# A selective scan with a mixture of experts: softplus by the logarithm, a share as a bias, and small products on two halves at once

## The chip, the cores and the metric

The kernel runs on one core of a Trainium2 chip. The metric is the time of one execution on the device in microseconds (us). A core has five engines that work side by side: PE (TensorE, matrix products), DVE (VectorE), ACT (ScalarE), POOL (GpSimd, here only issuing gathers and scatters) and SP (SyncE, issuing plain transfers). Each engine runs its own instructions in order; semaphores make one wait for another.

## The reference

The input x has 2 batches of 2048 tokens with 256 features. The result is x plus two branches of the normalised tokens. Cut to what matters:

```
xn = layernorm(x)
# branch 1: a scan over each batch's tokens, sorted by the nearest of 8 cluster means
prompt = (means @ prompt_weight.T)[bucket]         # 16 numbers per token
x_dbl  = x_proj_weight @ u                         # u: sorted tokens, (256, 2048); gives 32 + 16 + 16 rows
dts, Bm, Cm = x_dbl[:32], x_dbl[32:48], x_dbl[48:] + prompt.T
delta  = softplus(dt_projs_weight @ dts + bias)    # (256, 2048)
for t:                                             # 16 states n for each of 256 channels
    h = exp(delta[t] * A) * h + delta[t] * u[t] * Bm[t]
    y[t] = sum_n h * Cm[t] + D * u[t]
# branch 2: 8 experts, each token uses its best 2
probs = softmax(top-2 logits)
out = sum_k probs_k * (silu(xn @ w1[k]) * (xn @ w3[k])) @ w2[k]
```

Sorting is by a stable argsort of the bucket, so a batch's sorted tokens are eight runs, one per cluster.

## The kernel before

A front part loads x, takes statistics, scores each token against the means and the gate, normalises the rows, sorts, and writes the rows with their expert numbers and two shares to memory (`xn_d`, 260 columns: 256 features and four more). The first of the four is the best expert's number, the second the smaller share, the third the difference of the two shares.

Then two kinds of work run mixed.

**The scan** goes by eight *pieces* of 512 sorted steps (four per batch). For a piece, POOL gathers the rows (`gather`, four indirect transfers), PE transposes them into `u` (`turn`), and PE projects them: `project` (line 652) makes `px`, 64 rows by 512 steps, in two products over the halves of the 256 features, and `end_projection` (659) adds the prompts with a third one, from `member`, a table of 8 clusters by 512 steps that is 1 where the step is in the cluster's run (`find_members`, line 644, two DVE instructions). ACT copies `px` to `xd`; SP stores its last 32 rows to memory (`bc`) and later loads them spread over partitions (`load_b`, `load_z`). `step_size` (685) makes, for each half h of the channels, `pd` = 32-row product of 512 columns, and ACT takes |pd + bias|, relu(pd + bias) and exp(-|pd + bias|) from it. Softplus is relu + log(1 + e), and log(1 + e) is a product of four quadratic factors: ACT makes each square (`square`, 700) and DVE multiplies them up (`series`, 706: five instructions and one more for delta times u), 512 columns at a time, for each of two halves.

A piece has eight *steps* (4 groups of 4 states, times 2 halves of the channels), and a step has four *places*, one per state. At a place ACT makes `da` = exp(delta * A) of the step after (`decay`, six buffers), DVE makes `bu` and runs the scan (`hs`, three buffers); a step later PE transposes `hs` into `pt_s` (two PSUM banks, pool "t"), ACT copies it to `ht`, and PE contracts with `z` into `y`, four products side by side on four groups of 32 partitions.

**The experts** go by 71 *tiles* of 128 rows. POOL gathers weights (`load_up`, `load_down`) into three buffers and rows (`load_rows`) into `xg`, with four buffers: a buffer is written again when all that read it are done. `turn` (854) transposes the rows on PE, ACT copies them to `xT`, and DVE makes `own`, the tile's share per row, in two instructions: the difference where the tile's expert is the row's best, plus the smaller share. `up` makes two products of 16 pairs, ACT takes Tanh of the first, DVE does `silu` and `gate`, `down` makes `py`; ACT scales it by `own` into `yo` and POOL adds `yo` into memory (`add_rows`). The products `px`, `pd`, `pt_g`, `pt_u` and `py` share a PSUM pool "m" of two banks.

**The order** is written out: each engine keeps the order of the text. `at_place` (1029) puts the pieces' preparations at fixed places of the piece before, with costs in us for PE and DVE, and a loop over the places (1076) gives out the tiles' parts (`jobs`: up 0, up 1, and down of the tile before) wherever PE's sum falls behind DVE's. `part_down(t)` turns tile t+2, gathers rows for tile t+5, then does `down(t)` and loads weights for t+3. The first piece is prepared in a *lead* (1000), whose thirteen entries alternate with jobs. When all jobs are given, memory is copied to the output, and the last piece's sums are added to it.

Of the kernel before, what the change touches and what calls it, by code (L numbers as in the profile page):

```python
# [40 lines left out]
F32 = mybir.dt.float32  # L41
BF16 = mybir.dt.bfloat16
I32 = mybir.dt.int32
AF = mybir.ActivationFunctionType
ALU = mybir.AluOpType
# [4 lines left out]
P = 128  # L50
CH = 512
# [4 lines left out]
LOG1P = (  # L56
    (1.0093577, 1.1060627), (-0.08225194, 3.2574694), (-1.424736, 2.702104), (-2.321687, 0.43240654),
)
LOG1P_C = 0.0052326876


@with_exitstack
def scan_moe_kernel(
# [14 lines left out]
    nc = tc.nc  # L78
    B, L, D = x.shape
# [3 lines left out]
    R = dt_wT.shape[0]  # L83
# [9 lines left out]
    SH = 4  # L93
    BJ = B * J
# [26 lines left out]
    last = [cst.tile([K, NCH], F32, name=f"last{b}") for b in range(B)]  # L121
# [80 lines left out]
    log1p_a = cst.tile([P, len(LOG1P)], F32, name="log1p_a")  # L202
    for i, (a, _) in enumerate(LOG1P):
        nc.vector.memset(log1p_a[:, i : i + 1], a)
# [25 lines left out]
    dtT = cst.tile([R, D], F32, name="dtT")  # L230
    nc.sync.dma_start(dtT, dt_wT)
# [41 lines left out]
    def small_weights():  # L273

        diag = cst.tile([P, ND, P], F32, name="diag")
        for h in range(ND):
            nc.vector.tensor_scalar(diag[:, h, :], ident, dcol[:, h : h + 1], None, ALU.mult)

        cp = cst.tile([K, XP], F32, name="cp")
        nc.vector.memset(cp, 0.0)  # L280
        pc = ps_m.tile([K, NS], F32, tag="m", name="pc")
        for h in range(ND):
            nc.tensor.matmul(
                pc, lhsT=chosen_by[:, h, 0:K], rhs=pwT[:, h, :], start=h == 0, stop=h == ND - 1
            )
        nc.vector.tensor_copy(cp[:, R + NS :], pc)

        nc.scalar.activation(na, na, AF.Exp)
        nc.vector.tensor_scalar_mul(na, na, -1.0)
        return diag, cp  # L290
# [146 lines left out]
    def sort_tokens():  # L437
# [56 lines left out]
        for b in range(B):  # L494
            nc.vector.tensor_scalar(first[b], begins, fst[:, b : b + 1], None, ALU.add)
            nc.vector.tensor_scalar(last[b], first[b], cntT[:, b : b + 1], None, ALU.add)
# [129 lines left out]
    class Piece:  # L626
# [17 lines left out]
        def find_members(self):  # L644
            b, c = self.b, self.c
            self.member = scn.tile([K, CH], F32, tag="member", name="member", bufs=1)
            nc.vector.tensor_scalar(self.member, at, first[b][:, c : c + 1], None, ALU.is_ge)
            nc.vector.scalar_tensor_tensor(
                self.member, at, last[b][:, c : c + 1], self.member, ALU.is_lt, ALU.mult
            )  # L650

        def project(self, h: int):
            if h == 0:
                self.px = ps_m.tile([XP, CH], F32, tag="m", name="px")
            nc.tensor.matmul(  # L655
                self.px, lhsT=xpT[:, h, :], rhs=self.u[:, h, :], start=h == 0, stop=False
            )

        def end_projection(self):
            nc.tensor.matmul(self.px, lhsT=cp, rhs=self.member, start=False, stop=True)  # L660
            self.xd = prep.tile([XP, CH], F32, tag="xd", name="xd")
            nc.scalar.copy(self.xd, self.px)
            nc.sync.dma_start(bc_d[self.b][self.c], self.xd[R:XP, :])
# [21 lines left out]
        def step_size(self, h: int):  # L685

            if h == 0:
                self.e = pre.tile([P, ND, CH], F32, tag="tok", name="e")
                self.r = pre.tile([P, ND, CH], F32, tag="tok", name="r")
                self.sq = {}  # L690
            pd = ps_m.tile([P, CH], F32, tag="m", name="pd")
            nc.tensor.matmul(  # L692
                pd, lhsT=dtT[:, h * P : (h + 1) * P], rhs=self.xd[0:R, :], start=True, stop=True
            )
            nc.scalar.activation(self.e[:, h, :], pd, AF.Abs, bias=bias[:, h : h + 1])
            nc.scalar.activation(self.r[:, h, :], pd, AF.Relu, bias=bias[:, h : h + 1])  # L696

            nc.scalar.activation(self.e[:, h, :], self.e[:, h, :], AF.Exp, scale=-1.0)

        def square(self, h: int, i: int):  # L700
            self.sq[h, i] = scn.tile([P, CH], F32, tag="sq", name="sq", bufs=3)
            nc.scalar.activation(  # L702
                self.sq[h, i], self.e[:, h, :], AF.Square, bias=log1p_a[:, i : i + 1]
            )

        def series(self, h: int, i: int):

            if h == 0 and i == 0:
                self.dl = prep.tile([P, ND, CH], F32, tag="dl", name="dl")
                self.du = prep.tile([P, ND, CH], F32, tag="du", name="du")  # L710
            dl = self.dl[:, h, :]
            if i < len(LOG1P):
                nc.vector.scalar_tensor_tensor(
                    dl, self.sq.pop((h, i)), LOG1P[i][1], dl if i else self.e[:, h, :],
                    ALU.add, ALU.mult,
                )
            elif i == len(LOG1P):
                nc.vector.scalar_tensor_tensor(
                    dl, dl, LOG1P_C, self.r[:, h, :], ALU.mult, ALU.add
                )  # L720
            else:
                nc.vector.tensor_mul(self.du[:, h, :], dl, self.u[:, h, :])
# [107 lines left out]
    class Tile:  # L830
# [23 lines left out]
        def turn(self):  # L854
# [11 lines left out]
            nc.vector.tensor_add(self.own, self.own, xg[:, D + 1 : D + 2])  # L866
# [27 lines left out]
        def down(self):  # L894
# [6 lines left out]
            yo = ffn.tile([P, D], F32, tag="yo", name="yo", bufs=3)  # L901
            nc.scalar.activation(yo, py, AF.Copy, scale=self.own)  # L902
# [90 lines left out]
    def first_series(h: int):  # L993
        for i in range(len(LOG1P) + 2):
            if i < len(LOG1P):
                p.square(h, i)
            p.series(h, i)

# [5 lines left out]
        [lambda: p.load_b(0), *(lambda q=q: p.load_z(q) for q in range(NQ)), lambda: p.step_size(0)],  # L1004
        [lambda: p.step_size(1), lambda: first_series(0)], [lambda: first_series(1)],
# [29 lines left out]
    for n, p in enumerate(pieces):  # L1035
# [3 lines left out]
        if n:  # L1039
            s1 = s0 - SP_  # L1040
            at_place(max(s1 - 1, 0), 1 if n > 1 else 0, p.gather)
            for h in range(ND):
                at_place(s1 + 1, 2 + h, lambda p=p, h=h: p.turn(h), 0.5)
                at_place(s1 + 2, 1 + 2 * h, lambda p=p, h=h: p.project(h), 0.95)
                at_place(s1 + 3 + h, 2 - 2 * h, lambda p=p, h=h: p.step_size(h), 1.0)
                for i, place in enumerate(((17, 18, 20, 21, 23, 25), (19, 22, 24, 26, 28, 30))[h]):
                    if i < len(LOG1P):
                        at_place(s1, place - 2, lambda p=p, h=h, i=i: p.square(h, i))
                    at_place(s1, place, lambda p=p, h=h, i=i: p.series(h, i), 0.0, 0.6)
            at_place(s1 + 2, 0, p.find_members, 0.0, 1.2)  # L1050
            at_place(s1 + 3, 0, p.end_projection, 0.95)
# [117 lines left out]
```

## Time and profile before

| | |
|---|---|
| Time, median of 3 runs | 794.46 us (793.4 to 795.9) |
| Profiled execution | 793.45 us |
| Its span | 791.7 us |
| Mean granted TensorE clock | 0.951 |
| PE busy | 712.9 us, 90% |
| DVE busy | 711.3 us, 90% |
| ACT busy | 507.9 us, 64% |
| POOL busy | 520.9 us, 66% |

Busy time counts an instruction from start to end; neighbours overlap, so the distance of two starts is what one really takes from its engine. "Idle before" is the engine's wait just ahead of an instruction, with what ended it. The chain is followed back from the last instruction to what released each one. POOL's rows are issues of indirect transfers; the transfers land later.

The front part lasts to about 67 us, the lead to about 117, the mixed stretch to about 751, and the last scan steps, the copy and the last sums to 791.7.

### The profile page before, as it was taken

Reading aid. Unit: us, or ns where it says so; the run is one execution under the profiler, and the core shown is the slowest. Engines: PE = TensorE matmul, PEld = TensorE weight load, DVE = VectorE, ACT = ScalarE, POOL = GpSimd, SP = SyncE. Lnnn points to the kernel's source line nnn. Section 1 sums busy time; section 2 is a strip of 40 time slices with the busy share of each in tenths; the row PEclk is TensorE's granted clock in tenths of the full one; section 3 lists DMA queues with packets and bytes.
Section 4 is the critical chain, followed back from the end, with each engine's and each line's share of the span. In section 5 each row is a group of like instructions: output and inputs, shape, how many; then the busy total and the mean of one; then the engine's idle time right before and its main releaser. Section 6 shows DMA issues by size and latency. Waiting matters only on the chain.

```text
span 791.7 us, 16967 instructions
## 1 busy us (share of the span) xinstructions
PE 712.9 (90%) x6552; PEld 605.5 (76%) x6552; DVE 711.3 (90%) x1162; ACT 507.9 (64%) x986; POOL 520.9 (66%) x374
## 2 busy tenths in 40 slices
PE   7385979899999999899999999999999998999963
PEld 5144768589877988599868986798779885998842
DVE  8865269899999999899989999899999998899991
ACT  4821266586669657776668666866687576757572
POOL 2023738657867886788776787878678787686313
PEclk9755999999999999999999999999999998999996
DMA  8593244664368547855656367448644855444462
GB/s 280 222 323 114 58 173 108 210 172 97 108 155 244 154 106 215 203 148 143 206 140 176 56 247 219 107 95 263 197 111 132 273 156 112 107 102 96 86 219 27
DMA packets 61215, 125.90 MB, mean 159 GB/s; under 512 B 24464, under 2 KB 42032, under 8 KB 53776
## 3 DMA queue, kind: packets, MB, share of 16 engines
q0 software_dynamic: 40224, 65.03, 34.6%
q1 hardware_dynamic: 20912, 59.80, 22.1%
q8 instruction: 52, 0.85, 0.4%
q14 instruction: 27, 0.22, 0.1%
HBM read 180.06 MB, written 27.00 MB: 262 GB/s over the span
## 4 chain that ended last, share of the span: by engine, by line
PE 69%; ACT 6%; DVE 3%; issue 3%; DMA 2%; POOL 1%; POOLq 0%; SPq 0%; ACTq 0%; DVEq 0%
PE p_ps L875 28%; PE py L898 14%; PE pt_s L787 12%; PE y L796 6%; ACT ht L791 2%; DMA out_dram<-acc 2%; PE y L728 2%; PE pt_g L858 2%; PE px L655 2%; PE pd L692 1%; DVE hs L775 1%; ACT da L760 1%; DVE bu L766 1%; PE px L660 1%; PE pt_u L641 1%
## 5 line engine op out<-in xcount | busy, mean ns | idle before, releaser
L875 PE MATMUL p_ps<-xT,w 128*128 128x128 f32 x2272 | 280.3, 279 | 5.3 <-ACT sq L702 4.3
L875 PEld LDWEIGHTS p_ps<-xT,w 128*128 128x128 f32 x2272 | 268.2, 195 | 20.2 <-issue 9.3
L775 DVE TENSOR_TENSOR_SCAN hs<-da,carry,bu 128x512 f32<-128x512 f32 x192 | 246.2, 1283 | 0.0
L760 ACT ACTIVATE da<-dl,na 128x512 f32<-128x512 f32 x256 | 182.0, 723 | 1.1 <-DVE hs L775 1.0
L816 POOL DMA_INDIRECT acc<-yo,token_of x71 | 137.8, 1941 | 60.3 <-ACT yo L902 20.0
L766 DVE TENSOR_TENSOR bu<-du,bt 128x512 f32<-128x512 f32 x256 | 174.0, 680 | 0.0
L791 ACT COPY ht<-pt_s 128x512 f32<-128x512 f32 x256 | 137.1, 590 | 31.3 <-PE pt_s L787 31.0
L787 PE MATMUL pt_s<-ident,hs 128*128 128x128 f32 x1024 | 137.9, 279 | 14.7 <-ACT ht L791 8.7
L835 POOL DMA_INDIRECT w<-in_w_up_dram,w_row x71 | 94.8, 1335 | 84.2 <-DVE w_row L584 36.8
L898 PE MATMUL py<-w,g 128*128 128x256 f32 x568 | 139.0, 389 | 12.2 <-ACT r L696 8.7
L787 PEld LDWEIGHTS pt_s<-ident,hs 128*128 128x128 f32 x1024 | 117.7, 143 | 31.6 <-ACT ht L791 15.6
L898 PEld LDWEIGHTS py<-w,g 128*128 128x128 f32 x568 | 104.2, 193 | 27.1 <-ACT r L696 10.3
L849 POOL DMA_INDIRECT xg_sb<-xn,token_of x71 | 88.3, 1243 | 37.5 <-issue 30.2
L835 POOL DMA_INDIRECT w<-in_w_down_dram,w_row x71 | 93.5, 1317 | 21.6 <-issue 12.5
L883 ACT ACTIVATE t_sb<-p_ps 128x512 f32<-128x512 f32 x71 | 42.5, 599 | 69.4 <-PE p_ps L875 69.1
L902 ACT ACTIVATE yo<-py,own 128x256 f32<-128x256 f32 x71 | 33.8, 476 | 80.5 <-PE py L898 80.3
L775 DVE TENSOR_TENSOR_SCAN hs<-da,bu 128x512 f32<-128x512 f32 x64 | 78.2, 1223 | 0.0
L796 PE MATMUL y<-ht,z 128*32 128x128 f32 x2048 | 74.3, 279 | 2.5 <-ACT ht L791 1.9
L816 POOL DMA_INDIRECT acc<-yt,line_of x28 | 54.7, 1952 | 25.7 <-ACT ht L791 8.2
L796 PEld LDWEIGHTS y<-ht,z 128*32 128x32 f32 x2048 | 51.1, 110 | 24.5 <-issue 13.2
L888 DVE SCALAR_TENSOR_TENSOR t_sb<-t_sb,p_ps 128x512 f32<-128x512 f32 x71 | 48.2, 679 | 9.1 <-ACT t_sb L883 8.8
L892 DVE SCALAR_TENSOR_TENSOR g<-t_sb,p_ps 128x512 f32<-128x512 f32 x71 | 48.3, 681 | 7.2 <-PE p_ps L875 4.7
(188 smaller groups left out, 632.8 us busy)
## 6 DMA issues: line engine op xcount, KB each, us to landing
bt<-bc SPq DMA_DIRECT2D x32, 1024.0 KB, 5.4
z<-bc SPq DMA_DIRECT2D x32, 256.0 KB, 3.8
xn<-xt SPq DMA_DIRECT2D x8, 520.0 KB, 2.6
xt<-in_x_dram SPq DMA_DIRECT2D x8, 512.0 KB, 7.5
acc<-in_x_dram SPq DMA_DIRECT2D x8, 512.0 KB, 6.4
w<-in_w_up_dram,w_row POOLq DMA_INDIRECT x71
w<-in_w_down_dram,w_row POOLq DMA_INDIRECT x71
xg_sb<-xn,token_of POOLq DMA_INDIRECT x71
```

The lines of the kernel that those rows point to most:

```text
L760: nc.scalar.activation(self.da[i], self.piece.dl[:, self.h, :], AF.Exp, scale=na[:, self.h, n : n + 1])
L766: nc.vector.tensor_mul(self.bu[i], self.piece.du[:, self.h, :], self.piece.bts[self.q][:, i, :])
L775: nc.vector.tensor_tensor_scan(self.hs[:, :, i], self.da[i], self.bu[i], start, ALU.mult, ALU.add)
L787: nc.tensor.transpose(pt[:, j, :], self.hs[:, t0 : t0 + G, :].rearrange("p t n -> p (t n)"), ident)
L791: nc.scalar.copy(self.ht[i], pt)
L796: nc.tensor.matmul(p.ys[self.h][j * G : (j + 1) * G, i, :], lhsT=p.zs[q][:, i * (P // G) + j, :], rhs=self.ht[i][:, j, :], start=False, st ...
L816: ins = nc.gpsimd.indirect_dma_start(out=to, out_offset=bass.IndirectOffsetOnAxis(ap=numbers, axis=0), in_=rows, in_offset=None, compute_o ...
L835: nc.gpsimd.indirect_dma_start(out=to[self.t % NW], out_offset=None, in_=rows, in_offset=bass.IndirectOffsetOnAxis(ap=w_row[:, self.t : se ...
L849: nc.gpsimd.indirect_dma_start(out=self.xg, out_offset=None, in_=xn_d, in_offset=bass.IndirectOffsetOnAxis(ap=token_of[:, self.t : self.t ...
L875: nc.tensor.matmul(p[:, f, :], lhsT=wk[:, h, f * P : (f + 1) * P], rhs=self.xT[:, h, :], start=h == 0, stop=h == ND - 1,)
L892: nc.vector.scalar_tensor_tensor(self.g, self.s, 0.5, self.p3, ALU.mult, ALU.mult)
L898: nc.tensor.matmul(py, lhsT=self.g[:, f, :], rhs=w2[:, f, :], start=f == 0, stop=f == NH - 1)
```

## The change

- **Softplus.** The four squares and factors go. ACT makes w = 1 + e (`decay_of_one`), and log(w) for both halves in one instruction of 1024 columns (`log`). DVE takes the rounding of w, (w - 1) - e, from relu and adds the logarithm: four instructions of 1024 columns with the product with u.
- **The share.** The add to `own` moves from DVE in `turn` to ACT in `down`, as an Identity with the share from `xg` as bias.
- **Prompts by steps.** `member` is now 1 from the cluster's first step on, and the prompts' weights are differences of neighbouring clusters, so that the sum over the clusters begun is the prompt. One DVE instruction, and no `last`.
- **Two halves at once.** `px` is 128 partitions by 256: the first 256 steps in partitions 0 to 63, the second 256 in 64 to 127, each with its own products. `pd` becomes two tiles, one per half of the steps, each 128 by 2 by 256, read from `xd` at partitions 0 and 64 (`dtT` is loaded twice). Abs and Relu go by half of the steps and half of the channels, 256 columns each. `bc` is stored in two transfers.
- The planner's costs and places follow.

```diff
-    dtT = cst.tile([R, D], F32, name="dtT")
-    nc.sync.dma_start(dtT, dt_wT)
+    dtT = cst.tile([XP + R, D], F32, name="dtT")
+    for t in range(2):
+        nc.sync.dma_start(dtT[t * XP : t * XP + R, :], dt_wT)
...
+        differ = cst.tile([P, ND, K], F32, name="differ")
+        nc.vector.tensor_copy(differ[:, :, 0:1], chosen_by[:, :, 0:1])
+        nc.vector.tensor_sub(differ[:, :, 1:], chosen_by[:, :, 1:K], chosen_by[:, :, 0 : K - 1])
...
-            nc.vector.scalar_tensor_tensor(
-                self.member, at, last[b][:, c : c + 1], self.member, ALU.is_lt, ALU.mult
-            )
...
-                self.px = ps_m.tile([XP, CH], F32, tag="m", name="px")
-            nc.tensor.matmul(
-                self.px, lhsT=xpT[:, h, :], rhs=self.u[:, h, :], start=h == 0, stop=False
-            )
+                self.px = ps_m.tile([2 * XP, HC], F32, tag="m", name="px")
+            for t in range(2):
+                nc.tensor.matmul(
+                    self.px[t * XP : (t + 1) * XP, :], lhsT=xpT[:, h, :],
+                    rhs=self.u[:, h, t * HC : (t + 1) * HC], start=h == 0, stop=False,
+                )
...
+        def size_products(self):
+            self.pd = [ps_m.tile([P, ND, HC], F32, tag="m", name="pd") for _ in range(2)]
+            for h in range(ND):
+                for t in range(2):
+                    nc.tensor.matmul(
+                        self.pd[t][:, h, :], lhsT=dtT[t * XP : t * XP + R, h * P : (h + 1) * P],
+                        rhs=self.xd[t * XP : t * XP + R, :], start=True, stop=True,
+                    )
...
+            own = slice(t * HC, (t + 1) * HC)
+            for h in range(ND):
+                for to, f in ((self.e, AF.Abs), (self.r, AF.Relu)):
+                    nc.scalar.activation(to[:, h, own], self.pd[t][:, h, :], f, bias=bias[:, h : h + 1])
...
             nc.scalar.activation(self.e[:, h, :], self.e[:, h, :], AF.Exp, scale=-1.0)
-        def square(self, h: int, i: int):
...
+            nc.scalar.activation(self.w[:, h, :], self.e[:, h, :], AF.Identity, bias=ones[:, 0:1])
+        def log(self):
+            self.dl = prep.tile([P, ND, CH], F32, tag="dl", name="dl")
+            nc.scalar.activation(self.dl, self.w, AF.Ln)
+        def series(self, i: int):
+            if i == 0:
+                nc.vector.scalar_tensor_tensor(
+                    self.e, self.w, 1.0, self.e, ALU.subtract, ALU.subtract
+                )
+            elif i == 1:
+                nc.vector.tensor_sub(self.r, self.r, self.e)
+            elif i == 2:
+                nc.vector.tensor_add(self.dl, self.dl, self.r)
+            else:
                 self.du = prep.tile([P, ND, CH], F32, tag="du", name="du")
+                nc.vector.tensor_mul(self.du, self.dl, self.u)
...
-            nc.vector.tensor_add(self.own, self.own, xg[:, D + 1 : D + 2])
...
+            nc.scalar.activation(self.own, self.own, AF.Identity, bias=self.xg[:, D + 1 : D + 2])
             nc.scalar.activation(yo, py, AF.Copy, scale=self.own)
...
+            at_place(s1 + 3, 2, p.size_products, 1.1)
...
-                at_place(s1 + 2, 1 + 2 * h, lambda p=p, h=h: p.project(h), 0.95)
-                at_place(s1 + 3 + h, 2 - 2 * h, lambda p=p, h=h: p.step_size(h), 1.0)
...
+                at_place(s1 + 2, 1 + 2 * h, lambda p=p, h=h: p.project(h), 0.55)
+                at_place(s1 + 3, 2, lambda p=p, h=h: p.step_size(h))
+                at_place(s1, 16 + 2 * h, lambda p=p, h=h: p.decay_of_one(h))
+            at_place(s1, 20, p.log)
+            for i, place in enumerate((21, 22, 25, 26)):
+                at_place(s1, place, lambda p=p, i=i: p.series(i), 0.0, 1.1)
+            at_place(s1 + 2, 0, p.find_members, 0.0, 0.5)
+            at_place(s1 + 3, 0, p.end_projection, 0.55)
```

## The prediction

> **What bounds the kernel now.** I read busy shares, stretches, chain, waits, then PE's and POOL's order in time.
>
> ```profile
> PE 712.9 (90%) x6552; PEld 605.5 (76%) x6552; DVE 711.3 (90%) x1162; ACT 507.9 (64%) x986; POOL 520.9 (66%) x374
> ...
> PE 69%; ACT 6%; DVE 3%; issue 3%; DMA 2%; POOL 1%; POOLq 0%; SPq 0%; ACTq 0%; DVEq 0%
> ```
>
> ```profile
> 200.00:300.00 100.00, 97.64 (x966) 85.19 (x965) 97.80 (x140) 70.54 (x141) 78.37 (x51) 1.00 0.57 153
> ...
> 600.00:700.00 100.00, 96.10 (x921) 85.20 (x920) 95.23 (x140) 68.14 (x135) 78.23 (x53) 0.97 0.56 146
> ```
>
> From 120 to 750 us PE and DVE are both busy some 96% (columns: PE, PEld, DVE, ACT, POOL, then PE's clock). But the chain is 69% PE and 3% DVE. The timelines agree: in most steps PE starts the first transpose of `hs` 5 to 8 us after DVE ended its last scan. So PE sets the pace, and DVE follows close behind.
>
> ```profile
> PE py L898 <- ACT r L696: 8.7, 5, 3.1
> PE pt_s L787 <- ACT ht L791: 8.7, 13, 1.4
> ...
> DVE dl L713 <- ACT sq L702: 24.4, 7, 13.8
> ```
>
> PE's waits are short and end on ACT: `pd` holding both "m" banks, and `ht`. DVE's 24.4 us on the squares is 13.8 in the lead and 10.6 later, under PE's work.
>
> ```profile
> 235.58 1.07 PE L655 MATMUL px<-u,xpT 128*64 128x512 f32 x2
> 236.58 1.07 PE L660 MATMUL px<-member,cp 8*64 8x512 f32 x2
> 237.58 2.05 PE L875 MATMUL p_ps<-xT,w 128*128 128x128 f32 x16
> ...
> 253.00 1.89 PE L898 MATMUL py<-w,g 128*128 128x256 f32 x8
> 254.82 1.08 PE L796 MATMUL y<-ht,z 128*32 128x128 f32 x32
> 255.83 3.84 PE L875 MATMUL p_ps<-xT,w 128*128 128x128 f32 x32
> 259.50 1.04 PE L787 MATMUL pt_s<-ident,hs 128*128 128x128 f32 x8
> ```
>
> Differences of starts are PE's true price. Every fp32 matmul is two passes. A 512-wide pair takes 1.00 us; `py`, 256 wide, 1.82/8 = 0.23 a pass (0.216 at its best, 1.73 for 8 in the chain); `p_ps`, 128 wide, 3.67/32 = 0.115. But `y`, whose four outputs lie in four groups of 32 partitions, takes 1.01/32 = 0.032: matmuls on different columns of the array run side by side, 3.5 at a time out of 4, entry and exit included.
>
> **Part 1, projection and step sizes on PE.** Per piece go three 512-wide pairs for `px` and two for `pd`: 5 x 1.0 us. In come 20 passes of 256, in pairs on partitions 0 and 64. Side by side at `y`'s efficiency (3.5/4, so 1.75 of 2) they take 20 x 0.216/1.75 = 2.5 us. Bounds: one after the other 4.3, perfectly paired 2.2. `px` splits columns, as `y` does; `pd` splits rows (K = 32 at 0 and 64), which no row shows. I take 2.5, since `y` is nearest: 2.5 us saved per piece, on the path in seven pieces: **-17.5 us** (-5 to -20).
>
> Both `pd` tiles now take both "m" banks until eight Abs and Relu of 256 are done. The row for such a size is `yo` (476 ns, next start 0.37 later): 3.0 us instead of 1.2 for one bank at a time. In the built order a feed-forward product of 1.8 to 3.6 us stands behind `pd` in four of the seven pieces; in the other three come a 1.0 us contraction, `pt_g` and `py`, which wait about 2 us. That is 6 us against 8.7 now: **-2.5** (-8 to +6).
>
> **Part 2, the logarithm on ACT.**
>
> ```profile
> L713 DVE SCALAR_TENSOR_TENSOR dl<-sq,dl 128x512 f32<-128x512 f32 x48 | 32.2, 671 | 0.6
> ...
> L866 DVE TENSOR_TENSOR own<-own,xg_sb 128x1 f32<-128x1 f32 x71 | 11.3, 160 | 2.4
> ...
> L378 ACT ACT_TABLE_LOAD x1 | 1.3, 1283 | 0.7 <-PEq L1158 0.7
> ```
>
> DVE: 12 operations of 0.60 us (start to start) per piece become 4 of 1024, at most 1.2: 2.4 saved; the second membership test, 0.7, goes; the add to `own`, 11.3 in all, moves to ACT. That is 8 x 3.1 + 11 = 36 us off DVE. I count it at nothing: DVE is ahead of PE and is tied to it by `silu` and `gate`. If PE's waits vanished with it, 31 us (PE's start-to-start excess between 125 and 745 us) would be the most.
>
> ACT: 64 squares go (46 us); in come 16 Identity (11.6), 8 logarithms of 1024 (about 1.2 each, 9.6), 32 more Abs/Relu of half width (net +9), 71 adds of one column (13, by the 182 ns `carry` copy), and table loads: Tanh and Exp sit in one set, Ln in another, and the built order has 17 loads, not one. 16 x 1.28 = 20.5. ACT goes from 508 to about 525, far from a bound.
>
> What counts is the hole: load, Ln, load is 1.28 + 1.1 + 1.28 = 3.7 us in which no `ht` is copied, while PE has two "t" banks. I laid PE's order against ACT's from the last Tanh or `yo` before the load. Piece 2: ACT is through Tanh, `da`, hole, `da`, first `ht` at 6.1 us; PE has an up product (1.8), transposes (0.9), `pt_g` and `py` (1.95) before the next `pt_s`: 4.65, so 1.5 us lost. Piece 7: 6.5 against 4.5, so 2.0. The other five have 6.5 to 7.5 us of PE work and lose 0 to 0.2. Sum **+3.7**. Lower bound 0. Upper bound: if an engine must run empty before each switch for as long as the load itself, the hole grows by 2.6 and the seven lose 19.8. I take the single row, because it is the thing itself.
>
> The Trainium skill's page "ScalarE: Activation LUTs" (What ACT_TABLE_LOAD costs) counts 1283 ns for the load, as the row here, but about 2.66 us for every change of set, a drain included. By that rule the sum below would end some 16 us higher, slightly slower than before.
>
> The lead's ACT-DVE chain gets shorter: now Abs starts at 98.8 and the first `da` at 113.5, 14.7 us. After: 8 x 0.38, Exp and Identity twice (2.5), load 1.3, Ln 1.1, xT/own/yo 0.8, load 1.3, Tanh 0.5 = 10.5. With PE's 1.3 at `px`: -5.5.
>
> **Part 3, the second share as a bias.** The bias reads the gathered rows `xg` in `down`, not in `turn`. `xg` has four buffers, so the gather of tile t+4 now waits for ACT's add in `down(t)`, and POOL's queue waits behind it.
>
> ```profile
> 73.03 0.96 POOL L849 DMA_INDIRECT xg_sb<-xn,token_of  x1 [0.30 <-issue]
> 79.78 1.00 POOL L835 DMA_INDIRECT w<-in_w_up_dram,w_row  x1 [5.78 <-PE p_ps L875]
> ...
> 84.83 0.96 POOL L620 DMA_INDIRECT xs<-xn,line_of  x1 [0.30 <-issue]
> ```
>
> In the lead, the gather at 73.03 (tile 4) must wait for the add in front of `yo`(0), about 83.9. The first piece's four gathers sit behind it: last start 90.4, not 84.8, and PE's `pt_u` waits for them: **+5.5**. Against the -5.5 above the lead is even.
>
> ```profile
> 539.75 1.52 POOL L849 DMA_INDIRECT xg_sb<-xn,token_of  x1 [0.30 <-DMA acc<-yo,token_of]
> 541.57 1.60 POOL L816 DMA_INDIRECT acc<-yo,token_of  x1 [0.30 <-ACT ht L791]
> ...
> 551.08 1.00 POOL L835 DMA_INDIRECT w<-in_w_up_dram,w_row  x1 [0.30 <-PE pt_s L787]
> ```
>
> Later: tile 52's gather goes out at 539.75, `xT` before `yo`(48) ends at 544.7, so all behind it moves by 4.9 us. POOL has little to catch up with: only 59 us between 120 and 752 are idle beyond the 0.3 us behind every issue. Before the pieces' gathers the shifts are 8.6, 3.8, 4.3, 2.0, 4.9, 4.1; the gathers now land (1.85 after the last, by the lead's DMA wait) 2.9 to 9.8 us ahead of `pt_u`, so 1.6 us is lost in all, and about 3 where the up weights of tile 51 (551.08, used at 555.2) come late: **+5**. Bounds: 0, and 27.7 if each shift reaches PE in full. The 71 adds delay `yo` by 0.1 to 0.2 us each; little of it is on the path: **+1**.
>
> Left at nothing: the planner's lower costs for these steps, which move feed-forward parts by a place or two (the order built from the changed text, which I used above, holds this); prompts by steps (weights formed once, members one test, off the path); two stores of `bc` instead of one on SP (0.3 us of issue; loads of z follow at 2 us and more); one more small load at the start.
>
> **Sum.** -17.5 - 2.5 + 3.7 + 0 + 5 + 1 = -10. The profiled execution took 793.45 (span 791.7 and 1.75 around it), 1.0 below the median 794.46: **783.5 us**. About 0.3% (2.4 us) is what this kernel's measurement can tell from no change.
>
> **Rivals.** (A) The switch costs double: +16, **800 us**. For it: nothing shows ACT going on right after a load (the only one is followed by 4.68 us of waiting for PE). Against: the row says 1.28. It decides when each hole is some 2 us longer than 3.7. (B) POOL becomes the pace: three or four more shifts reach PE, +15, **798 us**. For it: four issues per tile are 7.0 us and feed-forward stretches run at 7.5 a tile. Against: the gate opens once per tile, and slacks of weights are mostly 10 us. (C) The halves do not run side by side: 20 x 0.216 = 4.3, +12, **795 us**, no change. Against: `y`. (D) DVE was the real co-bound, and half of PE's 31 us of excess goes too: **768 us**. For it: 96% busy. Against: 3% of the chain.
>
> The Trainium skill's "TensorEngine Tiling (Array Packing)" (Key Properties) says that changing the tiling mode drains TensorE. Here `y`'s 32 passes lose 0.1 us against perfect packing (1.01 against 32 x 0.112/4), entry and exit together; four such groups per piece would be 0.4 us, and the sum, by `y`'s efficiency, holds that already.
>
> **Chances.** Forecast 0.45 (its own range 775 to 791), A 0.25, B 0.1, C 0.08, D 0.12. Faster: 0.44 + 0.12 + 0.02 = 0.58; same: 0.01 + 0.02 of A, 0.02 of B, 0.04 of C = 0.09; slower 0.33. The range goes from D, 767, to past A's centre and B's, 806.
>
> **What would show it.** Right: `px` and `pd` groups of 0.5 us (start to start); table loads of 1.3 us with Ln next to them; the wait of `dl` on `sq` gone; DVE under 680 us busy; PE still most of the chain. Wrong: PE's waits on `ht` beyond 25 us, a gap behind each load (A); POOL waiting on `own` and PE on `xs`, `xg` or weights (B); `pd` passes starting 0.22 us apart (C); PE's waits all but gone (D).

## The result and the profile after

The changed kernel takes 824.31 us (median of 4 runs, 821.23 to 827.23) against 794.72 (4 runs) before: ratio 1.0372, 95% interval 1.0331 to 1.0414. It is 3.7% slower; the forecast was 783.5 us, faster, in a range that ended at 806. Ratios, here and below, are those measured over the fast runs of both kernels; they can differ by up to 0.3% from the quotient of the two medians. The profiled execution took 824.63 us, with a span of 822.9 (791.7 before). So 31 us are to be explained, and they came although nearly every instruction did what the forecast said. First the page's busy line:

```profile
PE 714.1 (87%) x6632; PEld 620.4 (75%) x6632; DVE 673.8 (82%) x1015; ACT 526.1 (64%) x1065; POOL 532.5 (65%) x374
```

DVE fell from 711 to 674 us and ACT rose from 508 to 526, as forecast. PE's sum did not fall: `px` and `pd` lose 18.8 us of busy time, but PE's clock was halved for longer (below), and products at half clock take longer; `p_ps` alone gains 9.2 us. Its timeline shows the halves at work (start, length, engine and line, tile):

```profile
675.94 0.65 PE L652 MATMUL px<-u,xpT 128*64 128x256 f32 x4
676.52 0.44 PE L870 MATMUL pt_g<-ident,xg_sb 128*128 128x128 f32 x2
```

Four passes of 256 columns in 0.58 us from start to start, where the same work took 1.0 before; in the trace the two passes of a pair start 7 ns apart, in `pd` as in `px`. Over the pieces after the lead, `px` and `pd` together go from 35.9 us of PE's time to 20.0: the 15.9 us are there. What does not follow is the span. The same two stretches as before, then the waits of PE, POOL and DVE (us in total, times, longest):

```profile
200.00:300.00 100.00, 94.89 (x938) 84.61 (x938) 91.30 (x118) 70.86 (x148) 77.33 (x50) 1.00 0.57 150
600.00:700.00 100.00, 87.44 (x807) 76.46 (x805) 78.17 (x102) 64.60 (x134) 77.10 (x51) 0.93 0.55 145
```

```profile
PE pt_u L638 <- DMA xs<-xn,line_of: 15.1, 9, 3.1
PE pt_s L799 <- ACT ht L803: 13.9, 14, 2.2
PE p_ps L886 <- ACT xT L872: 6.7, 3, 3.0
...
PE py L909 <- ACT r L709: 4.0, 4, 1.0
PE p_ps L886 <- ACT own L913: 3.7, 1, 3.7
PE py L909 <- DMA w<-in_w_down_dram,w_row: 3.0, 2, 2.3
```

```profile
POOL xg_sb L861 <- ACT own L913: 86.6, 26, 13.4
```

```profile
DVE t_sb L899 <- ACT t_sb L894: 73.7, 43, 6.3
```

Both PE and DVE are less busy between 600 and 700 us than before (96.1 and 95.2 then), so neither is the bound there: something keeps both waiting. The wait for `r` fell from 8.7 to 4.0 us; the forecast had 6. New are PE's 15.1 us for gathered rows `xs` (0.5 before; 5.1 of them lie in the lead), its waits for `xT` ahead of `p_ps` and for weights, and POOL's 86.6 us for ACT's add into `own`, which did not exist. DVE's wait for Tanh (`t_sb`) grows from 8.8 to 73.7 us: DVE has less to do, and Tanh follows PE's products.

Where the time is lost can be read by class. For each pair of neighbours on PE I took the distance of their starts, put it on the first, and summed by tile, from the end of the first step's last scan to the end of the very last scan (us; a wait thus lies with the instruction ahead of it):

| | before | after | six buffers | part 3 undone | no switch, part 3 undone |
|---|---|---|---|---|---|
| `px` and `pd` | 35.9 | 20.0 | 20.0 | 20.0 | 20.0 |
| `pt_u` | 7.1 | 20.0 | 7.1 | 10.4 | 12.0 |
| `py` | 121.2 | 131.2 | 131.4 | 130.9 | 120.8 |
| `y` | 91.1 | 99.6 | 96.3 | 95.0 | 96.5 |
| `p_ps` | 238.7 | 246.8 | 245.6 | 245.4 | 240.8 |
| `pt_s` and `pt_g` | 154.6 | 156.7 | 151.5 | 152.4 | 150.4 |
| whole stretch | 651.3 | 676.9 | 654.5 | 656.7 | 643.0 |

(The last three columns are experiments, below. The rest of a column, 2.6 us, is `pl`.) After minus before: -15.9 for the halves, and +12.9 at `pt_u`, +10.0 at `py`, +8.5 at `y`, +8.1 at `p_ps`. The lead adds 4.3.

### The profile page after: what moved, and what is told of

Same layout as the page of the kernel before. It is cut to its first block, busy times and chain, and to the rows that moved or that the text cites. A ratio compares the mean times of both kernels' runs of the same rounds, so it can differ in the third digit from the quotient of the medians.

```text
span 822.9 us, 16887 instructions
## 1 busy us (share of the span) xinstructions
PE 714.1 (87%) x6632; PEld 620.4 (75%) x6632; DVE 673.8 (82%) x1015; ACT 526.1 (64%) x1065; POOL 532.5 (65%) x374
## 5 line engine op out<-in xcount | busy, mean ns | idle before, releaser
L886 PE MATMUL p_ps<-xT,w 128*128 128x128 f32 x2272 | 289.5, 285 | 12.1 <-ACT xT L872 6.7
L886 PEld LDWEIGHTS p_ps<-xT,w 128*128 128x128 f32 x2272 | 277.0, 199 | 24.4 <-ACT xT L872 8.2
L861 POOL DMA_INDIRECT xg_sb<-xn,token_of x71 | 93.2, 1312 | 116.0 <-ACT own L913 86.6
L799 PEld LDWEIGHTS pt_s<-ident,hs 128*128 128x128 f32 x1024 | 119.3, 144 | 31.6 <-ACT ht L803 18.8
L899 DVE SCALAR_TENSOR_TENSOR t_sb<-t_sb,p_ps 128x512 f32<-128x512 f32 x71 | 48.5, 684 | 74.3 <-ACT t_sb L894 73.7
L808 PE MATMUL y<-ht,z 128*32 128x128 f32 x2048 | 78.3, 286 | 4.1 <-ACT ht L803 3.2
L914 ACT ACTIVATE yo<-py,own 128x256 f32<-128x256 f32 x71 | 33.7, 474 | 74.9 <-issue 51.4
L808 PEld LDWEIGHTS y<-ht,z 128*32 128x32 f32 x2048 | 52.4, 113 | 25.1 <-ACT ht L803 11.3
L828 POOL DMA_INDIRECT acc<-yt,line_of x28 | 57.0, 2035 | 14.3 <-issue 6.7
```

What stands on the lines that cost most here:

```text
L799: nc.tensor.transpose(pt[:, j, :], self.hs[:, t0 : t0 + G, :].rearrange("p t n -> p (t n)"), ident)
L808: nc.tensor.matmul(p.ys[self.h][j * G : (j + 1) * G, i, :], lhsT=p.zs[q][:, i * (P // G) + j, :], rhs=self.ht[i][:, j, :], start=False, st ...
L828: ins = nc.gpsimd.indirect_dma_start(out=to, out_offset=bass.IndirectOffsetOnAxis(ap=numbers, axis=0), in_=rows, in_offset=None, compute_o ...
L861: nc.gpsimd.indirect_dma_start(out=self.xg, out_offset=None, in_=xn_d, in_offset=bass.IndirectOffsetOnAxis(ap=token_of[:, self.t : self.t ...
L886: nc.tensor.matmul(p[:, f, :], lhsT=wk[:, h, f * P : (f + 1) * P], rhs=self.xT[:, h, :], start=h == 0, stop=h == ND - 1,)
L899: nc.vector.scalar_tensor_tensor(self.s, self.s, 1.0, self.p1, ALU.add, ALU.mult)
```

## The experiments

My theory after comparing the traces: the gate of part 3 (POOL's in-order queue stands behind a gather that waits for ACT's add) costs most. Rivals: the holes of the table loads (part 2), and ACT's 71 adds by themselves. Later two more questions came up: what a hole costs, and why the halves bring so little. Ratios are to runs of the kernel before on the same chip in the same session; before took 794.5 us (median) beside the first four runs, 795.1 beside the next four, 807.5 on the chip of the third four and 794.8 beside the last. Across chips only ratios are compared.

### The gate

```diff
 # six buffers, on the changed kernel
-            self.xg = ffn.tile([P, D + SH], F32, tag="xg", name="xg_sb", bufs=4)
+            self.xg = ffn.tile([P, D + SH], F32, tag="xg", name="xg_sb", bufs=6)
```

> The changed kernel with six buffers for `xg` instead of four, so that the gather of a tile's rows reuses the buffer of a tile whose add ended a step or more earlier. The gate theory (POOL's queue waits with a gather for ACT's add in `down`, and what stands behind it reaches PE late: 45 us lost, given 15 saved on PE): about 25 us come back, 795 to 803 us, POOL's 86.6 us of waiting for `own` nearly gone, PE's wait of `pt_u` for `xs` back from 15 to under 2 us. The hole theory (table loads hold up `ht` and `xT`): 817 to 825 us. The theory that ACT's 71 adds cost by themselves (308 ns each): 818 to 825 us.

Measured: 798.15 us, ratio 1.0023 (0.9983 to 1.0062). 27.7 us of 29.6 come back with two more buffers and nothing else.

```diff
 # part 3 alone, on the kernel before: turn(), down()
-            nc.vector.tensor_add(self.own, self.own, xg[:, D + 1 : D + 2])
...
+            nc.scalar.activation(self.own, self.own, AF.Identity, bias=self.xg[:, D + 1 : D + 2])
             nc.scalar.activation(yo, py, AF.Copy, scale=self.own)
```

> The kernel before with part 3 alone: the second share added by ACT in `down`, four buffers of `xg`, everything else as before. The gate theory: most of the loss shows here without the logarithm and the halves, 812 to 824 us, with POOL waiting some 80 us for `own`. The hole theory: 794 to 799 us. The adds by themselves: 798 to 806 us, and then no wait of PE for gathered rows.

Measured: 826.7 us, ratio 1.0383 (1.0315 to 1.0450), a little above what was expected: the whole loss, without logarithm or halves. Its waits, then those of the run with six buffers:

```profile
POOL xg_sb L849 <- ACT own L901: 102.1, 29, 15.6
...
PE pt_u L641 <- DMA xs<-xn,line_of: 18.5, 11, 3.3
...
PE py L897 <- DMA w<-in_w_down_dram,w_row: 3.6, 3, 2.0
```

```profile
PE pt_s L799 <- ACT ht L803: 14.1, 16, 2.2
PE p_ps L886 <- ACT xT L872: 6.7, 3, 3.0
```

With six buffers POOL's wait for `own` ahead of a gather and PE's wait for `xs` are gone from the list; the waits for `ht` and `xT` are those of the changed kernel, so they are not the gate's.

```diff
 # part 3 undone, on the changed kernel: the reverse of the diff above
```

> The changed kernel with part 3 undone: DVE adds the second share in `turn`, as before; the logarithm, prompts by steps and the halves stay. The gate theory: 783 to 798 us, since what is left are the halves (-15) and the hole (+4 to +15). The hole theory: 815 to 823 us. If the adds cost by themselves, this is well under the run with six buffers; if only the gate costs, the two are within 3 us.

Measured: 794.47 us, ratio 0.9989 (0.9961 to 1.0018). Against the run with six buffers, on the same chip, that is 0.34% or 2.7 us for ACT's adds themselves; the two intervals overlap, so this size is not clear of the spread.

```diff
 # the add on ACT, but in turn() behind the copy of xT; four buffers
         def turn(self):
+            nc.scalar.activation(self.own, self.own, AF.Identity, bias=xg[:, D + 1 : D + 2])
         def down(self):
-            nc.scalar.activation(self.own, self.own, AF.Identity, bias=self.xg[:, D + 1 : D + 2])
```

> The changed kernel with ACT's add of the second share moved from `down` to `turn`, right behind the copy of `xT`: still 71 Identity of one column on ACT, still four buffers of `xg`, but the last read of a tile's rows comes one product pair earlier. If it is the place of the read that costs (the gate), 795 to 803 us, as with six buffers, and POOL's wait for `own` under 15 us. If it is ACT's adds, or the number of buffers whatever is read where, 815 to 826 us.

Measured: 808.5 us against 807.54 on that chip, ratio 1.0020 (0.9981 to 1.0059), the same as with six buffers, and POOL's wait for `own` ahead of a gather of rows is gone. Four buffers suffice as long as a tile's last read comes early; the engine that adds hardly matters, the place of the read does.

How the gate works is plain in POOL's timeline of the changed kernel's lead (in brackets the idle time before, and what ended it):

```profile
71.70 0.96 POOL L861 DMA_INDIRECT xg_sb<-xn,token_of  x1 [0.30 <-issue]
86.06 0.96 POOL L861 DMA_INDIRECT xg_sb<-xn,token_of  x1 [13.39 <-ACT own L913]
87.33 1.00 POOL L847 DMA_INDIRECT w<-in_w_up_dram,w_row  x1 [0.30 <-issue]
88.64 0.95 POOL L617 DMA_INDIRECT xs<-xn,line_of  x1 [0.30 <-issue]
```

The second gather stands 13.4 us, and the first piece's four gathers start at 88.6 instead of 81.1. The same happens, mostly for less long, at 25 more of the 71 gathers of rows. From the start of a piece's last gather to PE's first `pt_u` there were 6.4 to 13.5 us before in the seven later pieces; after, there are 0.6 to 6.1; with six buffers 5.0 to 13.6. And PE in the last piece:

```profile
659.42 1.48 POOL L617 DMA_INDIRECT xs<-xn,line_of  x1 [0.30 <-issue]
```

```profile
661.44 0.38 PE L638 MATMUL pt_u<-ident,xs 128*128 128x128 f32 x2
664.92 0.33 PE L638 MATMUL pt_u<-ident,xs 128*128 128x128 f32 x1 [3.10 <-DMA xs<-xn,line_of]
666.88 0.48 PE L638 MATMUL pt_u<-ident,xs 128*128 128x128 f32 x1 [1.63 <-DMA xs<-xn,line_of]
667.29 1.94 PE L808 MATMUL y<-ht,z 128*32 128x128 f32 x32
669.15 1.12 PE L638 MATMUL pt_u<-ident,xs 128*128 128x128 f32 x4
670.06 5.08 PE L886 MATMUL p_ps<-xT,w 128*128 128x128 f32 x32
```

The last rows arrive 7.5 us after their issue began. PE waits for rows in three more pieces behind the lead, and the rows that it waited for came 5.3, 6.2 and 6.2 us after their own issue began (in the pieces from 131, 224 and 311 us). In the lead it was 2.7 to 2.9. And the wait is not all: the `p_ps` behind it took 5.08 us where 32 such passes take 3.8. The stretches of 5 us show why (columns as before, PE's granted clock third from the end):

```profile
660.00:665.00 5.00, 1.90 (x16) 1.47 (x15) 5.00 (x7) 2.48 (x5) 4.39 (x3) 1.00 0.73 234
665.00:670.00 5.00, 3.37 (x38) 2.48 (x39) 2.72 (x5) 1.21 (x2) 4.70 (x2) 0.60 0.14 41
670.00:675.00 5.00, 5.00 (x35) 5.00 (x34) 0.69 (x1) 2.49 (x5) 4.02 (x4) 0.71 0.59 131
```

After a wait of a few us PE's clock is often halved for a while. In the records these are stretches of 3.41 us, or two of them in a row, at 0.50; those of the changed kernel start at 140.38, 157.45, 188.17 us and so on, always whole multiples of 3.413 us apart. From 125 us to the last `y` the kernel before has 5 of them (8.5 us lost if PE works through all), the changed one 12 (20.5 us), six buffers 7 (11.9 us). In the changed kernel six stretches, one of them double, begin 0.4 to 1.1 us after the end of a PE wait of 1.9 to 3.1 us: for `xs` (ended at 139.9, 320.8 and 664.9), for `xT` (187.3 and 529.0) and for a down weight (607.1). A seventh follows a wait of 2.2 us for `ht` (713.4), two follow waits of 1.0 and 1.4 us, and two lie in the last scan steps. It is no fixed rule: with six buffers a wait of 2.98 us for `xT` (ended at 175.4) and one of 2.2 us for `ht` (684.1) had no such stretch behind them. The Trainium skill's "TensorE: Matmul & The Clock Gate" (What's actually happening) describes such a gate, half speed after an idle window of 3413 ns that runs free of the kernel; length, depth and the regular starts agree with the records here, but the waits here were shorter than that window.

### The table loads

```diff
 # no switch, on the changed kernel
-            nc.scalar.activation(self.dl, self.w, AF.Ln)
+            nc.scalar.activation(self.dl, self.w, AF.Identity)
```

> The changed kernel with the logarithm left out: the same operation of the same size as Identity, from the set that is already loaded (so the step sizes are not those of the reference), no table load after the first. The gate theory: 814 to 822 us, because the holes cost 4 to 8 us only. The hole theory: 795 to 806 us, with PE's waits for `ht` and `xT` back to those of before (8.7 and under 1 us). The adds by themselves: 814 to 822 us.

Measured: 808.07 us, ratio 1.0184 (1.0143 to 1.0225), some 15 us better than the changed kernel: more than the gate theory allowed for, less than the hole theory.

> The changed kernel with part 3 undone (DVE adds the second share in `turn`) and the logarithm left out (Identity in its place, so the step sizes are not those of the reference; no table load after the first). If the gate and the holes cost independently (30 and 16 us by the runs so far), this is 776 to 783 us. If the holes cost only because the gate had used up PE's cover, 788 to 795 us.

This is both edits at once, part 3 undone and Identity for the logarithm. Measured: 782.0 us, ratio 0.9858 (0.9800 to 0.9916). Against 0.9989 with the logarithm, the loads cost 1.3% or 10.4 us; by the two intervals this is uncertain by some 5 us. PE's waits show where: for `xT` ahead of `p_ps` 6.0 us with the logarithm and none without, for `ht` ahead of `pt_s` 13.3 and 10.4. One hole of the changed kernel, on ACT and then on PE:

```profile
181.58 1.28 ACT L720 ACT_TABLE_LOAD   x1
182.88 1.07 ACT L720 ACTIVATE dl<-w 128x1024 f32<-128x1024 f32 x1
183.95 1.28 ACT L772 ACT_TABLE_LOAD   x1
185.24 0.72 ACT L772 ACTIVATE da<-dl,na 128x512 f32<-128x512 f32 x1
185.87 1.05 ACT L803 COPY ht<-pt_s 128x512 f32<-128x512 f32 x2
186.81 0.38 ACT L872 COPY xT<-pt_g 128x256 f32<-128x256 f32 x1
```

```profile
182.16 0.38 PE L870 MATMUL pt_g<-ident,xg_sb 128*128 128x128 f32 x2
182.38 1.89 PE L909 MATMUL py<-w,g 128*128 128x256 f32 x8
187.25 2.97 PE L886 MATMUL p_ps<-xT,w 128*128 128x128 f32 x16 [2.98 <-ACT xT L872]
```

The load takes 1.28 us and the next instruction starts 0.01 to 0.02 us behind it, so the hole is the forecast's 3.7 us (181.58 to 185.24) and no drain adds to it. What it holds up is not only `ht`: the next up product needs `xT`, whose copy stands behind the hole, `da` and two `ht`. That is 3.0 us here and once more (at 529.0), with a halved clock behind it both times, and 0.8 us in a third piece of seven. In the table these 10 us lie at `py`, which stands ahead of the waiting product: 131 with the logarithm, 121 without.

Is it the length of the hole, or ACT's time? The split hole loads, in front of the logarithm, the set that holds Exp as well, so that the load back comes only at the next Tanh:

```diff
 # split hole, on the changed kernel with part 3 undone
+            nc.scalar.preload_act_table_set("natural_log_exp_and_others")
             nc.scalar.activation(self.dl, self.w, AF.Ln)
```

> The changed kernel with part 3 undone, and the logarithm's set loaded as the one that has Exp too, so that the load back comes at the next Tanh (in seven of eight pieces 2 to 10 operations of ACT later) and not right behind the logarithm: the same 17 loads, but holes of 2.4 and 1.3 us with `ht` and `xT` copies between them instead of one of 3.7. If a hole costs by its length beyond PE's cover: 783 to 789 us, and PE's waits for `ht` and `xT` about half of those in the run with part 3 undone. If the loads cost by ACT's time whatever their place: 793 to 797 us.

Measured: 790.43 us, ratio 0.9935 (0.9904 to 0.9966), against 0.9989: 4.3 us back with the same 17 loads, between the two expectations; the two intervals just overlap. PE's waits for `xT` ahead of `p_ps` fall from 6.0 to 3.1 us and those for `ht` from 13.3 to 12.7. So it seems that length counts, and for `xT` above all; the waits for `ht` were expected to halve and did not.

Without the halves:

```diff
 # logarithm alone: changed kernel, part 3 undone, px/pd/step_size of the kernel before
-                self.px = ps_m.tile([2 * XP, HC], F32, tag="m", name="px")
+                self.px = ps_m.tile([XP, CH], F32, tag="m", name="px")
...
-            self.pd = [ps_m.tile([P, ND, HC], F32, tag="m", name="pd") for _ in range(2)]
+            pd = ps_m.tile([P, CH], F32, tag="m", name="pd")
```

> The changed kernel with part 3 undone and projection and step sizes in one piece of 512 steps, as before; prompts by steps and the logarithm stay, with 16 table loads. If the logarithm costs what the halves bring (the run with part 3 alone undone stands level with the kernel before): 806 to 813 us. If neither moves the time: 793 to 797 us.

Measured: 789.61 us, ratio 0.9926 (0.9902 to 0.9950). Both expectations miss: it is faster than before, and faster than with the halves (0.9989), so with the logarithm the halves cost some 0.6%. By class the stretch behind the lead is 649.7 us here and 656.7 with the halves: -15.7 at `px` and `pd`, but +6.3 at `py`, +5.4 at `y`, +3.9 at `pt_g`, +3.7 at `pt_u` and +3.6 at `pt_s`.

Two more runs without the halves, one with Identity for the logarithm and one with the split hole:

> The logarithm's version without the halves and without part 3, with the logarithm left out again (Identity in its place, so the step sizes are not those of the reference; no table load after the first). With the halves the holes cost 10 us (794.5 against 782). If a hole costs the same here, 778 to 783 us, and DVE's relief alone brings 12 to 16 us. If PE's longer products for `px` and `pd` cover the holes, 786 to 790 us, and the relief brings 5 to 9.

> The logarithm's version without the halves and without part 3, with the split hole (the set with Exp and Ln at the logarithm, the load back at the next Tanh, which is next at once in two of the eight pieces). If its one hole costs some 10 us: 782 to 787 us. If PE's longer products cover the hole already: 788 to 792 us, no better than the unsplit one (789.6).

Both on the slower chip: 793.61 us, ratio 0.9848 (0.9796 to 0.9900), without switch; 795.84 us, ratio 0.9883 (0.9832 to 0.9934), with the split hole. By ratios the whole hole costs 0.8% here and half of it comes back by the split, but the unsplit run was on another chip, so this is an indication. Beside the same versions with the halves (0.9858 and 0.9935), the halves bring nothing in the first and cost 0.5% in the second.

### The halves

```diff
 # halves alone, on the kernel before: project, end_projection, size_products, step_size(t) as
 # in the change, exp per half h, then square() and series() by four factors as before
```

> The kernel before with projection, prompts and step sizes for two halves at once, and prompts by steps; step sizes by squares and series on DVE, the share added by DVE, as before. If part 1 is worth what PE's starts show (2.2 us per piece, 15.5 in all, and less waiting for `pd`'s banks): 775 to 783 us. If PE's saving is taken up by a wait for DVE, which has its 36 us back: 788 to 795 us.

Measured: 789.67 us, ratio 0.9945 (0.9912 to 0.9978): 4.4 us of the forecast 20, in the range of the second expectation. By class the stretch of 651.3 us loses 13.8 at `px` and `pd` and gains 6.2 at `p_ps`, 2.7 at `y`, 2.6 at `py` and less elsewhere: 646.6. Four more runs, on one chip, asked what gives the rest away.

```diff
 # short series, on the kernel before and on the halves alone
-    (1.0093577, 1.1060627), (-0.08225194, 3.2574694), (-1.424736, 2.702104), (-2.321687, 0.43240654),
+    (1.0093577, 1.1060627), (-0.08225194, 3.2574694),
```

> The kernel before with two of the four factors of the logarithm's series left out (so the step sizes are not those of the reference): 32 fewer operations on DVE (19 us) and 32 fewer squares on ACT, no table load, everything else as before. If DVE is one of the bounds of the kernel before: 1.0 to 1.6% faster than before. If PE alone sets the pace: within 0.4% of it.

> The halves, with the same short series (step sizes not those of the reference), no logarithm and no part 3. If DVE holds back what the halves save: 1.5 to 2.0% faster than the run with the short series alone. If POOL's queue or ACT's latency holds it back: within 0.7% of that run, as the halves' 0.55% without relief.

Measured: 786.13 us, ratio 0.9882 (0.9845 to 0.9920); with the halves 780.49 us, ratio 0.9831 (0.9801 to 0.9861). The relief alone brings 1.2% (9.4 us). The halves on top bring 0.5% again, so DVE, with this relief, does not hold them back. By class, from the one to the other: -16.6 at `px` and `pd`, +5.0 at `y`, +4.4 at `pt_u`, +1.8 at `py`.

```diff
 # fewer loads, on the kernel before and on the halves alone
-            self.fetch(w2_sb, down_rows)
+            if self.t < NW or self.t % 2 == 0:
+                self.fetch(w2_sb, down_rows)
```

> The kernel before with every second load of down weights left out from the fourth tile on (those tiles use the weights that lie in their buffer, so the sums are not the reference's): 34 fewer issues on POOL, some 60 us of its queue. If POOL's queue is one of the bounds of the kernel before: 0.6 to 1.2% faster than before. If not: within 0.4%.

> The halves alone with every second load of down weights left out in the same way (sums not the reference's). If POOL's queue holds back what the halves save: 1.5 to 2.0% faster than the run with fewer loads alone. If DVE or ACT's latency holds it back: within 0.7% of that run.

Measured: 800.6 us, ratio 1.0076 (1.0046 to 1.0106); with the halves 791.09 us, ratio 0.9945 (0.9927 to 0.9963). POOL's queue does not bound the kernel before: its idle time beyond the 0.3 us behind each issue goes from 62 to 115 us and no wait of PE changes by more than 0.1. Yet the run is slower, and no wait explains it. Between 120 and 150 us PE does the same in both (before, then with fewer loads); then a double stretch of half clock falls into the next 50 us of the one and not of the other:

```profile
120.00:150.00 30.00, 26.79 (x246) 22.52 (x245) 27.51 (x50) 16.50 (x33) 24.81 (x18) 1.00 0.49 137
150.00:200.00 50.00, 48.78 (x452) 42.69 (x451) 49.18 (x76) 35.43 (x71) 31.55 (x24) 1.00 0.54 153
```

```profile
120.00:150.00 30.00, 26.71 (x245) 22.43 (x244) 27.55 (x49) 16.50 (x33) 24.89 (x17) 1.00 0.54 151
150.00:200.00 50.00, 48.77 (x431) 41.99 (x429) 46.14 (x71) 34.91 (x69) 25.48 (x18) 0.93 0.45 118
```

Every piece ends 3.2 to 3.5 us after its counterpart, from the first to the last, so these 50 us are the whole difference up to there (all four runs lie within 1.1 us at the same mean clock, 0.945, so it is not one odd execution); the other 3.5 us of the two spans lie behind the last scan, where the output is stored. Against this run the halves bring 1.3%, between the two expectations, but in the profiled executions 0.4% of it is that stretch. And with fewer loads the halves take what they take with all loads (0.9945 both), so POOL's queue does not hold them back. So under neither relief do the halves bring what PE saves; what remains is that PE, sooner done, waits for ACT's copies (`ht`, `xT`), for the gathers, and at half clock. That is read from the classes; no run took ACT's latency away, so it is not shown further.

### A version that beats both

```diff
 # early gather, on the split hole's version
-            at_place(max(s1 - 1, 0), 1 if n > 1 else 0, p.gather)
+            at_place(s1 - 2 if n > 1 else 0, 3 if n > 1 else 0, p.gather)
```

> The version with the split hole, and each later piece's four gathers of rows two places earlier on POOL. In that version PE waits for `xs` once or twice (2.7 us at most) and TensorE's clock is halved for some 3.4 us after such waits. If these late gathers hold PE back: 783 to 788 us, with no wait of `pt_u` for `xs`. If POOL's queue only hands the delay to the weights and adds behind the gathers: 789 to 794 us, with PE waiting for weights instead.

Measured: 798.89 us on the slower chip, ratio 0.9898 (0.9862 to 0.9934), with 0.5 us left of PE's wait for `xs`. With the split logarithm alone (0.9883), it is about 1% faster than the kernel before and 4.6% faster than the changed one. Which of the two is better can't be told; the one with the split logarithm alone leaves the halves out, and no run here shows them to be worth keeping beside the logarithm.

## Why the prediction was wrong, point by point

Four kernels lead from the one to the other in steps, each read as a ratio times 794.5 us, since not all ran on one chip; by the intervals a step is known to some 4 to 5 us. Beside it stands what the sum had for the same step:

| step | from, to | measured | the sum |
|---|---|---|---|
| halves, DVE's relief, shorter lead, no loads | 1 to 0.9858 | -11.3 | -17.5 - 2.5 + 0 - 5.5 = -25.5 |
| table loads | 0.9858 to 0.9989 | +10.4 | +3.7 |
| share added by ACT, rows free in time | 0.9989 to 1.0023 | +2.7 | +1 |
| gather gated by four buffers | 1.0023 to 1.0372 | +27.7 | +5.5 + 5 = +10.5 |
| together | 1 to 1.0372 | +29.5 | -10.3, given as -10 |

- **The step that failed most: "Later ... +5", with "+5.5" in the lead.** The mechanism was the forecast's, gate and queue; its size was off nearly threefold, 27.7 us where the sum had 10.5. The gathers lost 3.5 to 7.8 us of their lead over `pt_u` in the seven later pieces, not far above the forecast's shifts of 2.0 to 8.6. What was wrong is "the gathers now land (1.85 after the last, by the lead's DMA wait)": that row comes from a stretch where the DMA engines were busy 0.33 of the time (60 to 100 us), and the pieces' gathers land where it is 0.57 (200 to 300 us). The rows that PE waited for there came 5.3 to 7.5 us after the start of their issue (2.8 in the lead), so what was counted as 2.9 to 9.8 us of reserve was gone in four pieces. That the busier DMA makes the landing longer is likely, but no run shows it by itself. Outside the lead the gate costs some 19 us, inside the bounds of 0 and 27.7; the value taken was near the wrong end. (That the whole also measured 27.7 is chance, for the bound left the lead out.)
- **Waits were counted at their face value.** PE waits 15.1 us for `xs`, and `pt_u` loses 12.9 outside the lead, yet the gate costs 27.7. Against six buffers, by class: 8.5 in the lead (end of the first step's scan at 128.7 and 120.2), 12.9 at `pt_u`, and 9.5 spread over `y`, `pt_s`, `pt_g` and `p_ps`. (That is 30.9 in these two executions, whose spans differ by 32.2.) Outside the lead the waits for `xs` make 10.0 us of these 22.4, the waits for weights 4.4 more than with six buffers, and five more stretches of half clock 8.6, which together nearly closes. The profile before had shown the last: clock 0.97 between 600 and 700 us, where PE waits 3.1 us for `r`.
- **Part 1, "-17.5 ... on the path in seven pieces".** PE's price was right (15.9 us saved; 0.58 us per group against the 0.5 forecast), "on the path" was not: alone the halves bring 4.4 us, on the short series 0.5%, and with the logarithm nothing or less (0.9926 without them, 0.9989 with them). What takes the saving up stays open: the short series speaks against DVE, the fewer loads against POOL's queue, and ACT's copies were not tested. A chain that is 69% PE says that PE was last at each step, not that the next engine is far behind. Rival C, halves that do not run side by side, is refuted: the pairs start 7 ns apart.
- **DVE's relief, "I count it at nothing".** Measured 9.4 us by the short series (which takes 23 us off ACT too, so the two are not told apart). The logarithm without loads and without the halves, which has all of the relief and the shorter lead, gives 0.9848, or 12.1 us: the first row of the table is about that, with nothing left for the halves. Rival D had the right place; its time was for a sum that stopped there.
- **The lead.** -5.5 without the gate: measured -3.6 at the first step with part 3 undone, and +4.3 with the gate, forecast "even".
- **Part 2, "+3.7".** The load's price was right, and rival A's drain does not exist here; the Trainium skill's "ScalarE: Activation LUTs" (What ACT_TABLE_LOAD costs) has 2.66 us for a change of set, the trace 1.283 and the next instruction 0.02 later. The step that failed laid only `ht` behind the hole. PE's next up product waits there for `xT` too, 3 us in two pieces and 0.8 in a third, with the clock behind it: 10.4.
- **The adds** take 308 ns each, not 182. The idle time ahead of `yo` did not grow by them (80.5 us before, 74.9 after); in time they are worth some 2.7 us, not clear of the spread.
- **Rival B** (POOL becomes the pace) named the right waits, POOL for `own` and PE for `xs` and weights. Its price for the gate, 15 us above the sum's 10.5, was nearly what was measured; its time of 798 us was not, because the halves and the loads in the same sum were off.

## What to carry to other kernels

Moving a tile's last read later is a change to its buffer, not to arithmetic: find who refills the buffer, and everything queued behind that refill, and if it can't read early, add a buffer. Take a transfer's landing time from the stretch where it must land, since a quieter stretch may show half of it (2.8 us here, against 5.3 to 7.5). A wait of two or three us on TensorE may cost another 1.7 us by the clock, so a sum of waits can fall well short of the loss. And a saving on the engine that leads the chain can be worth far less than its size: 15.9 us of PE's time brought 4.4 here.

## What was not expected of the hardware

- Half-clock stretches of 3.41 us come or stay away in schedules that are equal to 0.1 us (1.00 against 0.93 in the same 50 us), worth 3.4 us, or 0.4% of this kernel.
- Six of the versions spread over 9 to 11 us in 9 or 10 runs (six buffers: 791.2 to 801.8), the kernel before over 8 in 19. The clock does not explain all of it: four runs with six buffers had the same mean clock, 0.945, and took 791.2, 791.5, 792.2 and 801.6 us.
- The same kernel before took 794.5 to 795.1 us on three chips and 807.5 on a fourth.
- An ACT table load costs 1.283 us and no more: where it need not wait for its operand, the instruction behind it starts within 0.02 us, and the one ahead ends within 0.02 us.
- A one-column Identity with a bias per partition takes ACT 308 ns, where a copy of four columns takes 182.
